# Seven query blocks of 476 instead of six of 496 and one of 351, with the block end and the projections moved to other steps

## Chip, cores, metric

One core of one Trainium2 chip. The time is device time in microseconds of one launch, the median of three runs: 10464.55 (10460.74 to 10472.15). Five engines work beside each other, each with its own queue in program order: TensorE (PE in the profile, PEld for its weight loads), VectorE (DVE), ScalarE (ACT), GpSimd (POOL) and SyncE (SP), which here only issues transfers. They meet at semaphores.

## What is computed

Two layers of a graph network on 3327 nodes with 128 features; `adj` is a dense 3327 x 3327 matrix of zeros and ones. Layer 0 (normalise, aggregate over `adj`, two linear maps, batch norm) takes the first 260 us. Layer 1 takes all the rest:

```
h = relu(layernorm(x))
q, k, v = (h @ Wq.T), (h @ Wk.T), (h @ Wv.T)       each reshaped to (128, 3327, 8)
a = einsum('dnh,dmh->dnm', q, k) * scale + adj + adj
out = softmax(a, axis=2) @ v                        for each of the 128 d
x = x + out.reshape(3327, 1024) @ Wo.T
```

So there are 128 batches (d) of an attention with 3327 queries n, 3327 keys m and a head width of only 8. The exponentials, 128 x 3327 x 3327 of them, are the bulk of the work.

## The kernel before

**Tiles.** Keys lie on the 128 partitions in 26 chunks (`NC`), queries along the free axis. Four batches (`G`) make a group, 32 groups in all. A group goes through seven query blocks (`qblocks`): six of `QB` = 496 queries and one of 351. A block goes through 13 steps (`SU`), numbered 0 to 12. A step handles four pairs; a pair is one key chunk for two of the four batches. Over a block that is 52 pairs.

**A pair** starts with a product on TensorE (`product`, L727): two matmuls of 32 contracted rows, written to one PSUM tile `s` of two banks. There are three such tiles in rotation. Then it goes one of two ways:

- *plain* (36 of 52): VectorE adds the adjacency tile `at` (L837, `d<-at,s`), and ScalarE takes the exponential of all plain pairs of a step in one instruction (`late`, L879, `d<-d`), issued in the next step behind that step's first exponential;
- *weighted* (16 of 52): ScalarE takes the exponential straight from PSUM (L846, `f<-s`), and GpSimd multiplies it by a tile `wt` of exponentials of the adjacency (L849), which were made once and lie in the DRAM tensor `wd`. The tiles `f` rotate over five buffers (pool `exf`).

A step has three plain pairs and one weighted; in the three steps of `DOUBLE` = (1, 6, 10) it has two of each. In the step after such a step the first product of the following step is issued early (`coming`).

**Weighing.** Three steps later (`LAG`) the four results of a step are multiplied with v on TensorE (L610, `av<-d,v` and `av<-f,v`, 16 matmuls, half of them in `second(0)`, half in `second(1)`) and summed into one of two accumulator banks `av`, used by the blocks in turn.

**The order inside a step** is written out by hand in the loop: first weighted exponential, `late()` of the step before, first add, `second(0)`, `step()`, second add, third add or second weighted pair (there also `begin`), `second(1)`, `go_on`.

**Block end.** The last weighing of a block is issued in step 2 of the next one. From there `step()` drives the generator `finish` by one piece a step: in step 3 VectorE copies the bank to `avs` (L618); in step 4 TensorE transposes it in four matmuls (L625), back into the same bank; in step 5 VectorE forms the reciprocal of the sums and multiplies (L632, L633, L635); in step 6 SP stores the result to `att`.

**Projections and outputs.** While group i runs, the q, k and v of group i + 2 are made in six parts and the output rows of group i - 1 in three. `begin` issues the matmul (L207) or the transposes (L268) or the last matmuls (L276) of one part in each double step, into the bank that is free; `go_on` issues VectorE's copy of it (L213, L233, L235, L270, L281) at the end of the same step, and the store a step later. GpSimd splits q and k in two (L236, L237). Groups 30 and 31 have no projections, group 0 has two sets of them and no output.

**Transfers.** All loads of `at` and `wt` are issued on SP two steps ahead (`fetch`), together with q, k, v of the next group and, in group 0, with the loads and stores that make `wd` for the next block (`more_weights`). Before the first block SP stores x to `xd` (L597) and h to `hd` (L549).

Of the kernel before, what the change touches and what calls it, by code (L numbers as in the profile page):

```python
# [9 lines left out]
F32 = mybir.dt.float32  # L10
# [3 lines left out]
ALU = mybir.AluOpType  # L14
# [4 lines left out]
N = 3327  # L19
D = 128  # L20
H = 8
P = 128
NC = 26
T = N * D
NP = NC * P
NB = 512
QB = 496
G = 4
EPS = 1e-5
HALF = 0.5 / math.sqrt(D)  # L30
# [2 lines left out]
WC = 18  # L33
CH = 4 * NP // D
NG = D // G
DOUBLE = (1, 6, 10)

# [8 lines left out]
def tile_two_layer_gnn(  # L46
# [17 lines left out]
    nc = tc.nc  # L64
# [3 lines left out]
    }))  # L68
    blocks = [(n0, min(NB, N - n0)) for n0 in range(0, N, NB)]

    qblocks = [(n0, min(QB, N - n0)) for n0 in range(0, N, QB)]

    const = ctx.enter_context(tc.tile_pool(name="const", bufs=1))
    dram = ctx.enter_context(tc.tile_pool(name="dram", bufs=1, space=DRAM))
# [10 lines left out]
    v1 = dram.tile([TP, H + 1], F32, name="v1")  # L85
    att = dram.tile([TP, H], F32, name="att")

    wd = dram.tile([NC - WC, P, N], F32, name="wd")
    xd = dram.tile([NP, D], F32, name="xd")
    hd = dram.tile([P, NP], F32, name="hd")  # L90

# [3 lines left out]
    attb = att[:T].rearrange("(d n) h -> d n h", n=N)  # L95
# [23 lines left out]
    LAG = 3  # L119
# [168 lines left out]
    def drive(part, bank=None):  # L288

        if bank is not None:  # L290
            next(part)
            part.send(bank)
        else:
            next(part, None)


    with tc.tile_pool(name="l0", bufs=1) as l0, tc.tile_pool(
        name="l0adj", bufs=3
    ) as ap, tc.tile_pool(name="l0s", bufs=2) as sp, tc.tile_pool(
        name="l0last", bufs=1  # L300
# [124 lines left out]
        for c in range(NC):  # L425
# [16 lines left out]
            i = c - 2 * NQ - 5  # L442
# [80 lines left out]
        def relu(i):  # L523
            n0, w = blocks[i]
            s = slice(n0, n0 + w)
            nc.scalar.activation(A2[:, s], A2[:, s], AF.Relu, bias=shift, scale=scale)

        def residual(i):
            pt, cs = turned(i, A, acc[i])
            nc.vector.tensor_add(xs[:, cs, :], xs[:, cs, :], pt)  # L530

        def second_norm(i, engine):

# [80 lines left out]

    def finish(rp, av, d0, n0, w):

        avs = rp.tile([P, NB], F32, name="avs")
        nc.vector.tensor_copy(avs[:, :w], av[:, :w])  # L618
        yield

        J = 4 if w == QB else 3
        R = w // J
        pt = av.rearrange("p (j q) -> p j q", j=4)
        for j in range(J):
            nc.tensor.transpose(  # L625
                pt[:R, j, :], avs[:, j : j + (R - 1) * J + 1 : J], ident
            )
        yield
        pv = pt.rearrange("p j (b h) -> p b j h", h=32)
        ri = rp.tile([P, G, 4], F32, name="ri")  # L630

        nc.vector.tensor_scalar(ri[:R, :, :J], pv[:R, :, :J, H], 1e-30, None, ALU.max)  # L632
        nc.vector.reciprocal(ri[:R, :, :J], ri[:R, :, :J])  # L633
        o = rp.tile([P, G, 4, H], F32, name="oq")
        nc.vector.tensor_tensor(  # L635
            o[:R, :, :J, :],
            pv[:R, :, :J, :H],
            ri[:R, :, :J].unsqueeze(3).to_broadcast([R, G, J, H]),
            ALU.mult,
        )  # L640
        yield
        nc.sync.dma_start(
            attb[bass.ds(d0, G), n0 : n0 + w, :].rearrange(
                "b (p j) h -> p b (j h)", j=J
            ),
            o[:R, :, :J, :].rearrange("p b j h -> p b (j h)"),
        )

    def rows_of(c):
        return min(P, N - c * P)  # L650

    def attention():


        with tc.tile_pool(name="adj", bufs=4) as ap, tc.tile_pool(
            name="adw", bufs=3
        ) as wp, tc.tile_pool(name="wk", bufs=2) as wk, tc.tile_pool(
            name="exf", bufs=5
        ) as fp, tc.tile_pool(name="exd", bufs=4) as ep, tc.tile_pool(
            name="res", bufs=2  # L660
        ) as rp, tc.tile_pool(name="psc", bufs=3, space=PSUM) as psc, tc.tile_pool(
# [7 lines left out]
            if True:  # L669
# [35 lines left out]
                def fetch(x):  # L705
                    while wanted and wanted[0][0] <= x:
                        _, kind, i, y, c = wanted.pop(0)
                        n0, w = qblocks[y]
                        if kind:
                            a = wp.tile([P, NB], F32, name="wt")  # L710
                            nc.sync.dma_start(a[:, :w], wd[c - WC, :, n0 : n0 + w])
                        else:
                            a = ap.tile([P, 2, NB], F32, name="at")
                            n = min(2, WC - 2 * c)
                            nc.sync.dma_start(
                                a[:, :n, :w], adjr[:, 2 * c : 2 * c + n, n0 : n0 + w]
                            )
                        have[kind, i, y, c] = a

                def product(i, y, c, half):  # L720
                    q, k, _ = sets[i % 2]
                    n0, w = qblocks[y]
                    we = w + w % 2
                    p = psc.tile([P, 2, NB], F32, name="s")
                    for x in range(2):
                        rs = slice(64 * half + 32 * x, 64 * half + 32 * x + 32)
                        nc.tensor.matmul(  # L727
                            p[:, x, :we], k[rs, c, :], q[rs, n0 : n0 + we],
                            start=True, stop=True,
                        )  # L730
                    return p
# [8 lines left out]
                def more_weights(i, y, s):  # L740

                    k, phase = s // 3, s % 3
                    if i or y + 1 >= len(qblocks) or k > 3:
                        return
                    n0, w = qblocks[y + 1]
                    c = WC + 2 * k
                    n = min(2, NC - c)
                    if phase == 0:
                        have["w"] = wk.tile([P, 2, NB], F32, name="t4")
# [65 lines left out]
                for x, (i, y, s) in enumerate(steps):  # L815
# [15 lines left out]
                    d = ep.tile([P, 3, 2, NB], F32, name="d")  # L831
                    es = [d[:, j] for j in range(len(plain))]

                    def add(j, p):
                        c = plain[j][0]

                        nc.vector.scalar_tensor_tensor(  # L837
                            d[:, j, :, :w],
                            have[0, i, y, c // 2][:, c % 2, :w]
                            .unsqueeze(1).to_broadcast([P, 2, w]),  # L840
                            SAFE / 2, p[:, :, :w], ALU.min, ALU.add,
                        )

                    def weighted(c, p):
                        f = fp.tile([P, 2, NB], F32, name="f")
                        nc.scalar.activation(  # L846
                            f[:, :, :w], p[:, :, :w], AF.Exp, scale=2.0
                        )
                        nc.gpsimd.tensor_tensor(  # L849
                            f[:, :, :w], f[:, :, :w],  # L850
                            have[1, i, y, c][:, :w].unsqueeze(1).to_broadcast([P, 2, w]),
                            ALU.mult,
                        )
                        es.append(f)
# [40 lines left out]
    def attention_shifted():  # L895

        with tc.tile_pool(name="shq", bufs=1) as shp, tc.tile_pool(
# [11 lines left out]
            with tc.For_i(0, D, G) as d0:  # L909
# [3 lines left out]
                for b in range(G):  # L913
# [2 lines left out]
                        sT[:, bass.ds((d0 + b if b else d0) * N, N)],  # L916
                    )
                for y, (n0, w) in enumerate(qblocks):
                    we = w + w % 2
                    av = avs2[y % 2]  # L920
                    waiting = []
# [166 lines left out]
```

## Time and profile before

| | |
|---|---|
| median of three runs | 10464.55 us |
| the profiled execution, its own time | 10472.29 us |
| its span, first to last instruction | 10470.4 us |
| granted TensorE clock, mean | 0.988 |
| first weighted exponential | 259.9 us |
| group 0, from there | 415.5 us |
| groups 1 to 31 | 311 to 317 us each |
| from the last step's first exponential to the end | 26.8 us |

Busy records of TensorE are modelled and those of ScalarE and VectorE overlap a little, so lengths are best read from start to start. In a timeline row, the first number is the start, the second the time from the first start to the last end of the merged instructions, `xN` their count, and the bracket says how long the engine had idled before it and who ended that. A group's row has busy time, mean ns of one, then the idle time in front.

### The profile page before, as it was taken

Reading aid. Unit: us, or ns where it says so; the run is one execution under the profiler, and the core shown is the slowest. Engines: PE = TensorE matmul, PEld = TensorE weight load, DVE = VectorE, ACT = ScalarE, POOL = GpSimd, SP = SyncE. Lnnn points to the kernel's source line nnn. Section 1 sums busy time; section 2 is a strip of 40 time slices with the busy share of each in tenths; the row PEclk is TensorE's granted clock in tenths of the full one; section 3 lists DMA queues with packets and bytes.
Section 4 is the critical chain, followed back from the end, with each engine's and each line's share of the span. In section 5 each row is a group of like instructions: output and inputs, shape, how many; then the busy total and the mean of one; then the engine's idle time right before and its main releaser. Section 6 shows DMA issues by size and latency. Waiting matters only on the chain.

```text
span 10470.4 us, 188308 instructions
## 1 busy us (share of the span) xinstructions
PE 9899.3 (95%) x72399; PEld 2827.8 (27%) x72399; DVE 9326.7 (89%) x9501; ACT 10000.4 (96%) x6655; POOL 8421.2 (80%) x4315
## 2 busy tenths in 40 slices
PE   7899999999999999999999999999999999999998
PEld 3222222222222222222222222222222222222222
DVE  5689999999999999999989999999999999999988
ACT  4799999999999999999999999999999999999998
POOL 1678888888888888888888888888888888888887
PEclk9899999999999999999999999999999999999999
DMA  6665666665666665666655666665666656666554
GB/s 229 207 176 157 166 168 165 164 164 159 163 168 164 167 163 156 165 170 166 166 160 156 167 170 166 163 163 156 169 169 165 165 158 161 168 168 165 158 154 127
DMA packets 1118973, 1735.29 MB, mean 166 GB/s; under 512 B 197582, under 2 KB 1094732, under 8 KB 1110380
## 3 DMA queue, kind: packets, MB, share of 16 engines
q1 hardware_dynamic: 1113678, 1718.96, 60.3%
q8 instruction: 568, 9.31, 0.4%
q10 hardware_dynamic: 4350, 4.20, 0.1%
q14 instruction: 345, 2.83, 0.1%
q0 software_dynamic: 32, 0.00, 0.0%
HBM read 1620.53 MB, written 102.30 MB: 165 GB/s over the span
## 4 chain that ended last, share of the span: by engine, by line
PE 36%; POOL 19%; DVE 18%; ACT 13%; issue 10%; DMA 1%; SPq 0%; ACTq 0%; DVEq 0%; POOLq 0%
PE av L610 18%; POOL f L849 18%; DVE d L837 16%; PE s L727 15%; ACT f L846 9%; ACT d L879 4%; PE av L625 1%; DVE avs L618 1%; POOL o L237 1%; PE av L276 1%; DMA wt<-wd 1%; DVE ri L633 0%; DMA t<-in_adjT 0%; PE av L207 0%; POOL o L236 0%
## 5 line engine op out<-in xcount | busy, mean ns | idle before, releaser
L837 DVE SCALAR_TENSOR_TENSOR d<-at,s 128x992 f32<-128x992 f32 x8064 | 8781.5, 1140 | 963.8 <-PE s L727 686.5
L849 POOL TENSOR_TENSOR f<-f,wt 128x992 f32<-128x992 f32 (+1 forms) x3584 | 7926.0, 2229 | 1786.2 <-ACT f L846 1749.5
L879 ACT ACTIVATE d<-d 128x2976 f32<-128x2976 f32 (+1 forms) x2912 | 7010.3, 2407 | 101.5 <-DVE d L837 97.0
L610 PE MATMUL av<-d,v 128*9 128x496 f32 x32256 | 5094.2, 569 | 0.8 <-ACT d L879 0.8
L727 PE MATMUL s<-q,k 32*128 32x496 f32 x23296 | 4260.4, 477 | 505.0 <-DVE d L837 259.2
L846 ACT ACTIVATE f<-s 128x992 f32<-128x992 f32 (+1 forms) x3584 | 3382.9, 966 | 166.8 <-PE s L727 85.4
L727 PEld LDWEIGHTS s<-q,k 32*128 32x128 f32 x23296 | 1786.6, 182 | 5767.2 <-DVE d L837 3267.4
L610 PE MATMUL av<-f,v 128*9 128x496 f32 x14336 | 2862.6, 568 | 0.0
L610 PEld LDWEIGHTS av<-d,v 128*9 128x9 f32 x32256 | 583.9, 88 | 1306.7 <-issue 1291.6
L610 PEld LDWEIGHTS av<-f,v 128*9 128x9 f32 x14336 | 316.8, 88 | 153.9 <-issue 148.0
L191 POOL CAST k<-ks 128x256 fp32r<-128x256 f32 x434 | 283.5, 653 | 0.0
L429 PE MATMUL acc<-a,A 128*128 128x512 f32 (+1 forms) x364 | 151.5, 569 | 23.3 <-ACT A L363 23.0
L625 PEld LDWEIGHTS av<-ident,avs 128*124 128x124 f32 (+1 forms) x864 | 122.4, 208 | 178.8 <-issue 177.5
L237 POOL TENSOR_TENSOR o<-pf,o 104x512 fp32r<-104x512 f32 x124 | 159.9, 1289 | 9.9
L625 PE MATMUL av<-ident,avs 128*124 128x128 f32 (+1 forms) x864 | 165.0, 312 | 0.6 <-DVE avs L618 0.6
L618 DVE COPY avs<-av 128x496 f32<-128x496 f32 (+1 forms) x224 | 144.8, 646 | 3.5 <-PE av L610 3.5
L436 DVE TENSOR_REDUCE amax<-a 128x1 f32<-128x3327 f32 x26 | 93.7, 3612 | 35.4 <-DMA a<-in_adj 35.2
L429 PEld LDWEIGHTS acc<-a,A 128*128 128x128 f32 x364 | 69.0, 192 | 108.2 <-issue 84.4
L402 POOL TENSOR_TENSOR sq<-wk 128x512 f32<-128x512 f32 x2 | 2.1, 1040 | 102.2 <-PE aside L403 102.2
L433 ACT ACTIVATE junk<-a 128x3327 bf16<-128x3327 f32 x26 | 77.4, 2977 | 6.6 <-DMA a<-in_adj 6.5
L236 POOL CAST o<-pf 104x512 fp32r<-104x512 f32 x124 | 76.3, 615 | 0.0
L635 DVE TENSOR_TENSOR oq<-av,ri 124x128 f32<-124x128 f32 (+1 forms) x224 | 64.2, 287 | 7.7
(120 smaller groups left out, 958.8 us busy)
## 6 DMA issues: line engine op xcount, KB each, us to landing
at<-in_adjT SPq DMA_DIRECT2D x1728, 496.0 KB
wt<-wd SPq DMA_DIRECT2D x1536, 248.0 KB
at<-in_adjT SPq DMA_DIRECT2D x288, 351.0 KB
ks<-kT SPq DMA_DIRECT2D x496, 104.0 KB
q<-qT SPq DMA_DIRECT2D x496, 104.0 KB
wt<-wd SPq DMA_DIRECT2D x256, 175.5 KB
a<-in_adj SPq DMA_DIRECT2D x26, 1663.5 KB
kT<-o SPq DMA_DIRECT2D x128, 208.0 KB
```

The source lines that it names most:

```text
L191: nc.gpsimd.tensor_copy(k[:, c : c + n, half * 64 : half * 64 + 64], ks.bitcast(F32).rearrange("g (p c) -> g c p", c=NC)[:, c : c + n, :],)
L237: nc.gpsimd.tensor_tensor(o[:CH, 1], f[:CH], o[:CH, 0].bitcast(F32), ALU.subtract)
L276: nc.tensor.matmul(bank[:CH, :D], tT[:, e, :CH], wo[:, e, :], start=(e == 0), stop=(e == H - 1))
L429: nc.tensor.matmul(acc[i][:, :w], A[:, c, :], a[:, n0 : n0 + w], start=(c == 0), stop=(c == NC - 1),)
L610: nc.tensor.matmul(av[32 * b : 32 * b + H + 1, :w], tiles[2][:, b, c, :], e, start=first, stop=last,)
L618: nc.vector.tensor_copy(avs[:, :w], av[:, :w])
L625: nc.tensor.transpose(pt[:R, j, :], avs[:, j : j + (R - 1) * J + 1 : J], ident)
L727: nc.tensor.matmul(p[:, x, :we], k[rs, c, :], q[rs, n0 : n0 + we], start=True, stop=True,)
L837: nc.vector.scalar_tensor_tensor(d[:, j, :, :w], have[0, i, y, c // 2][:, c % 2, :w] .unsqueeze(1).to_broadcast([P, 2, w]), SAFE / 2, p[:, ...
L846: nc.scalar.activation(f[:, :, :w], p[:, :, :w], AF.Exp, scale=2.0)
L849: nc.gpsimd.tensor_tensor(f[:, :, :w], f[:, :, :w], have[1, i, y, c][:, :w].unsqueeze(1).to_broadcast([P, 2, w]), ALU.mult,)
L879: nc.scalar.activation(flat, flat, AF.Exp, scale=2.0)
```

## The change

`QB` becomes 476, so that all blocks have it but the last, which is 472 wide and reaches over the 3327 queries to the padded 3328; the tiles of the attention shrink from 512 to 476 columns. `exf` has six buffers. `DOUBLE` is (3, 7, 11). `step()` is called in the steps of `PARTS` = (3, 5, 7, 8) only, after all products of the step: copy in step 3, transposes in step 5, reciprocal in step 7, store in step 8. `begin` is called in steps 7 and 11 alone, behind `second(1)`, and its bank is that of the other block. `finish` always works with four interleaved columns; the last block stores its last three rows on their own. In layer 0 x is stored to `xd` in three pieces, two of them earlier, and h to `hd` from GpSimd's queue. The adjacency's transpose is padded in both directions.

```diff
-QB = 496
+QB = 476
...
-DOUBLE = (1, 6, 10)
+DOUBLE = (3, 7, 11)
+PARTS = (3, 5, 7, 8)
...
-    qblocks = [(n0, min(QB, N - n0)) for n0 in range(0, N, QB)]
+    qblocks = [(n0, min(QB, NP - n0)) for n0 in range(0, NP, QB)]
...
-    wd = dram.tile([NC - WC, P, N], F32, name="wd")
+    wd = dram.tile([NC - WC, P, NP], F32, name="wd")
...
+        def keep_nodes(cs):
+            nc.sync.dma_start(
+                xd.rearrange("(c p) d -> p c d", p=P)[:, cs, :], xs[:, cs, :]
+            )
+
         def residual(i):
             pt, cs = turned(i, A, acc[i])
             nc.vector.tensor_add(xs[:, cs, :], xs[:, cs, :], pt)
+            if i < 2:
+                keep_nodes(cs)
...
             s = slice(4 * i0 * P, min(NC, 4 * i1) * P)
-            nc.sync.dma_start(hd[:, s], B2[:, s])
+            nc.gpsimd.dma_start(hd[:, s], B2[:, s])
...
-        nc.sync.dma_start(xd.rearrange("(c p) d -> p c d", p=P), xs)
+        keep_nodes(slice(8, NC))
         keep_columns(0, NQ)
...
     def finish(rp, av, d0, n0, w):
 
-        avs = rp.tile([P, NB], F32, name="avs")
-        nc.vector.tensor_copy(avs[:, :w], av[:, :w])
+        J = 4
+        R = -(-w // J)
+        avs = rp.tile([P, QB], F32, name="avs")
+        nc.vector.tensor_copy(avs[:, : R * J], av[:, : R * J])
         yield
 
-        J = 4 if w == QB else 3
-        R = w // J
...
+        r, j = divmod(min(w, N - n0), J)
         nc.sync.dma_start(
-            attb[bass.ds(d0, G), n0 : n0 + w, :].rearrange(
+            attb[bass.ds(d0, G), n0 : n0 + r * J, :].rearrange(
                 "b (p j) h -> p b (j h)", j=J
             ),
-            o[:R, :, :J, :].rearrange("p b j h -> p b (j h)"),
+            o[:r].rearrange("p b j h -> p b (j h)"),
         )
+        if j:
+            nc.sync.dma_start(
...
-            name="exf", bufs=5
+            name="exf", bufs=6
...
                 def begin(i, y, s):
-                    if extra:
+                    if extra and s in DOUBLE[1:]:
                         begun.append(extra.pop(0))
-                        drive(begun[0], avs2[(i * len(qblocks) + y + (s > LAG)) % 2])
+                        drive(begun[0], avs2[(i * len(qblocks) + y + 1) % 2])
...
                     second(0)
-                    step()
                     add(1, product(i, y, *plain[1]))
                     if len(rest) > 1:
                         weighted(rest[1][0], product(i, y, *rest[1]))
-                        begin(i, y, s)
                     else:
                         add(2, product(i, y, *plain[2]))
-
-                    if s - 1 in DOUBLE:
+                    if s in PARTS:
+                        step()
+
+                    if s - 1 in DOUBLE and x + 1 < len(steps):
                         coming = first(x + 1)
                     second(1)
+                    begin(i, y, s)
                     go_on(i, y, s)
...
-        "adjT": padded(adj.T),
+        "adjT": np.pad(adj.T, (0, NP - N)),
```

More of the change, by code (lines that the diff above doesn't have):

```diff
@@ L615, in finish @@
     def finish(rp, av, d0, n0, w):
-        avs = rp.tile([P, NB], F32, name="avs")
-        nc.vector.tensor_copy(avs[:, :w], av[:, :w])
+        J = 4
+        R = -(-w // J)
+        avs = rp.tile([P, QB], F32, name="avs")
+        nc.vector.tensor_copy(avs[:, : R * J], av[:, : R * J])
         yield
-        J = 4 if w == QB else 3
-        R = w // J
-        pt = av.rearrange("p (j q) -> p j q", j=4)
+        pt = av.rearrange("p (j q) -> p j q", j=J)
         for j in range(J):
@@ L629, in finish @@
         pv = pt.rearrange("p j (b h) -> p b j h", h=32)
[L630 to L634, printed above, removed]
+        ri = rp.tile([P, G, J], F32, name="ri")
+        nc.vector.tensor_scalar(ri[:R], pv[:R, :, :, H], 1e-30, None, ALU.max)
+        nc.vector.reciprocal(ri[:R], ri[:R])
+        o = rp.tile([P, G, J, H], F32, name="oq")
         nc.vector.tensor_tensor(
-            o[:R, :, :J, :],
-            pv[:R, :, :J, :H],
-            ri[:R, :, :J].unsqueeze(3).to_broadcast([R, G, J, H]),
+            o[:R], pv[:R, :, :, :H], ri[:R].unsqueeze(3).to_broadcast([R, G, J, H]),
             ALU.mult,
@@ L641, in finish @@
         yield
+        r, j = divmod(min(w, N - n0), J)
         nc.sync.dma_start(
-            attb[bass.ds(d0, G), n0 : n0 + w, :].rearrange(
+            attb[bass.ds(d0, G), n0 : n0 + r * J, :].rearrange(
                 "b (p j) h -> p b (j h)", j=J
             ),
-            o[:R, :, :J, :].rearrange("p b j h -> p b (j h)"),
+            o[:r].rearrange("p b j h -> p b (j h)"),
         )
+        if j:
+            nc.sync.dma_start(
+                attb[bass.ds(d0, G), n0 + r * J : n0 + r * J + j, :].rearrange(
+                    "b (o j) h -> o b (j h)", o=1
+                ),
+                o[r : r + 1, :, :j, :].rearrange("p b j h -> p b (j h)"),
+            )
     def rows_of(c):
@@ L709, in fetch @@
                         if kind:
-                            a = wp.tile([P, NB], F32, name="wt")
+                            a = wp.tile([P, QB], F32, name="wt")
                             nc.sync.dma_start(a[:, :w], wd[c - WC, :, n0 : n0 + w])
                         else:
-                            a = ap.tile([P, 2, NB], F32, name="at")
+                            a = ap.tile([P, 2, QB], F32, name="at")
                             n = min(2, WC - 2 * c)
@@ L748, in more_weights @@
                     if phase == 0:
-                        have["w"] = wk.tile([P, 2, NB], F32, name="t4")
+                        have["w"] = wk.tile([P, 2, QB], F32, name="t4")
                         nc.sync.dma_start(
@@ L830, in attention @@
                     plain, rest = pairs(s)
-                    d = ep.tile([P, 3, 2, NB], F32, name="d")
+                    d = ep.tile([P, 3, 2, QB], F32, name="d")
                     es = [d[:, j] for j in range(len(plain))]
@@ L844, in weighted @@
                     def weighted(c, p):
-                        f = fp.tile([P, 2, NB], F32, name="f")
+                        f = fp.tile([P, 2, QB], F32, name="f")
                         nc.scalar.activation(
@@ L918, in attention_shifted @@
                 for y, (n0, w) in enumerate(qblocks):
+                    w = min(w, N - n0)
                     we = w + w % 2
```

## The prediction

> **What bounds the kernel now.** I read the engines' shares first, then the costliest groups, then the timelines of ScalarE, VectorE and TensorE through one block of 496 queries.
>
> ```profile
> PE 9899.3 (95%) x72399; PEld 2827.8 (27%) x72399; DVE 9326.7 (89%) x9501; ACT 10000.4 (96%) x6655; POOL 8421.2 (80%) x4315
> ...
> L837 DVE SCALAR_TENSOR_TENSOR d<-at,s 128x992 f32<-128x992 f32 x8064 | 8781.5, 1140 | 963.8 <-PE s L727 686.5
> L849 POOL TENSOR_TENSOR f<-f,wt 128x992 f32<-128x992 f32 (+1 forms) x3584 | 7926.0, 2229 | 1786.2 <-ACT f L846 1749.5
> L879 ACT ACTIVATE d<-d 128x2976 f32<-128x2976 f32 (+1 forms) x2912 | 7010.3, 2407 | 101.5 <-DVE d L837 97.0
> L846 ACT ACTIVATE f<-s 128x992 f32<-128x992 f32 (+1 forms) x3584 | 3382.9, 966 | 166.8 <-PE s L727 85.4
> ```
>
> Three engines stand above 89%, so shares do not decide. The busy time of ScalarE's two groups adds to 10393 us, more than its 10000: records overlap, and what counts is the distance from start to start.
>
> ```profile
> 5322.45 1.00 ACT L846 ACTIVATE f<-s 128x992 f32<-128x992 f32 x1
> 5323.32 2.70 ACT L879 ACTIVATE d<-d 128x2976 f32<-128x2976 f32 x1
> 5325.90 1.01 ACT L846 ACTIVATE f<-s 128x992 f32<-128x992 f32 x1
> 5326.77 2.71 ACT L879 ACTIVATE d<-d 128x2976 f32<-128x2976 f32 x1
> 5329.35 1.91 ACT L846 ACTIVATE f<-s 128x992 f32<-128x992 f32 x2
> 5331.10 1.90 ACT L879 ACTIVATE d<-d 128x1984 f32<-128x1984 f32 x1
> 5332.88 1.01 ACT L846 ACTIVATE f<-s 128x992 f32<-128x992 f32 x1
> ...
> 5343.74 0.98 ACT L846 ACTIVATE f<-s 128x992 f32<-128x992 f32 x1
> 5345.13 2.69 ACT L879 ACTIVATE d<-d 128x2976 f32<-128x2976 f32 x1 [0.41 <-DVE d L837]
> ```
>
> A plain step (three adds) takes 3.45 us (5322.45 to 5325.90) for two exponentials of 3968 elements; a step with two adds, which I call double, has a second exponential on GpSimd's side and takes 4.33 (5325.90 to 5330.23: the row at 5329.35 merges this second one and the first of the next step, 0.88 later); the step after it 2.65 here, 2.63 at best. Nothing idles: ScalarE is the bound. A block without loss is 7 x 3.454 + 3 x 4.33 + 3 x 2.635 = 45.1 us. The block starts in this timeline (5089.66, 5135.50, 5182.30, 5228.63, 5276.04, 5322.45, 5368.58, 5404.84) give 45.8, 46.8, 46.3, 47.4, 46.4, 46.1 and 36.3: 315.2 us a group. So some 12 us a group are lost, and the last lines show how: the exponential of step 5 waits for VectorE.
>
> ```profile
> 5321.79 6.67 DVE L837 SCALAR_TENSOR_TENSOR d<-at,s 128x992 f32<-128x992 f32 x6
> 5329.12 1.19 DVE L837 SCALAR_TENSOR_TENSOR d<-at,s 128x992 f32<-128x992 f32 x1 [0.66 <-PE s L727]
> 5330.96 3.50 DVE L837 SCALAR_TENSOR_TENSOR d<-at,s 128x992 f32<-128x992 f32 x3 [0.65 <-PE s L727]
> 5334.38 0.67 DVE L618 COPY avs<-av 128x496 f32<-128x496 f32 x1
> 5334.96 3.38 DVE L837 SCALAR_TENSOR_TENSOR d<-at,s 128x992 f32<-128x992 f32 x3
> ```
>
> Adds follow each other after 1.098 us, so a plain step takes VectorE 3.29 of ScalarE's 3.45: 0.16 to spare. The copy of the block end (0.58 start to start) stands in plain step 3, the reciprocal's three instructions (0.70: 5342.07 to 5342.77) in plain step 5. Neither fits: steps 4 and 6 of this block take 3.85 and 4.86 instead of 3.45 and 4.33, and step 5 3.53. That is 1.0 us a block. After the double step VectorE idles 0.66 and 0.65.
>
> **The change, part by part.**
>
> *Width.* Columns of a group go from 3327 to 3328, with the same number of instructions. Per plain step ScalarE saves 8 x 20 elements; the 351 block's plain step (5371.79 to 5374.28, 2.49; 2.51 in others) against 3.454 gives 145 x 8 elements in 0.95 us, so 0.82 ns an element. Plain 3.454 - 0.13 = 3.32, double 4.33 - 0.167 = 4.164, after it 2.63 - 0.10 = 2.53; a block 7 x 3.32 + 3 x 4.164 + 3 x 2.53 = 43.35, seven less 0.35 for the last (472 wide) 303.05. The old widths without loss: 6 x 45.1 + 32.7 = 303.3. So width alone gives nothing; the gain can only be the 12 us of losses.
>
> [...]
>
> *Block end.* The copy moves to step 3, the reciprocal to step 7, both double now, after two adds. At 476 VectorE ends the second add 2.40 after the step's first exponential and gets the next step's product at about 3.0 (3.22 at 496). The copy (0.57) fits; the reciprocal's 0.70 ends at 3.10, and the second idle time of 0.65 takes the 0.1. Cost 0, against 1.0 before. Without this cover it would be 0.57 + 0.70 a block.
>
> The four transposes move from step 4 to step 5, behind that step's last product.
>
> ```profile
> 5337.57 0.73 PE L625 MATMUL av<-ident,avs 128*124 128x128 f32 x4
> 5338.23 0.50 PE L727 MATMUL s<-q,k 32*128 32x496 f32 x4
> ```
>
> They hold TensorE 0.66 from start to start. The step's last product waits for the exponential of its own step and starts 1.15 after this (5351.23 to 5352.39 in step 8; 1.12 at 476), takes 0.41, then come the weighing (0.95 from 5323.93 to 5324.88; 0.91 at 476) and the product for step 6, whose reader starts 0.53 after it (5330.42 to 5330.96): 1.12 + 0.41 + 0.91 + 0.53 = 2.97 of 3.32, 0.35 free. With 0.66 more, ScalarE waits 0.31. Seven blocks: 2.2 us a group. Bounds 0 (TensorE catches up) and 0.66.
>
> *Projections and outputs* (nine parts a group) start only in steps 7 and 11, now behind the last weighing. All write the other accumulator bank. In step 7 that bank is read by the reciprocal's last instruction in the same step, so in the changed program the projection's matmul carries a wait for VectorE; in step 11 it carries none. Behind it on TensorE stand the next step's first two products, and for them wait ScalarE and VectorE. Today's rows for matmul and copy:
>
> ```profile
> 5159.07 1.10 PE L207 MATMUL av<-wq,hj 128*104 128x512 f32 x2
> 5160.11 0.59 PE L610 MATMUL av<-d,v 128*9 128x496 f32 x2
> ...
> 5160.42 0.75 DVE L235 TENSOR_SCALAR pf<-av,low_half 104x512 f32<-104x512 f32 x1
> ```
>  Step 7, from its first exponential: second add until 2.40, reciprocal's end 3.18, matmul 3.24 to 4.27 (1.04 from 5159.07 to 5160.11), product of step 8 to ScalarE at 4.83 instead of 4.17: 0.66 late. VectorE's copy starts 1.35 after the matmul at 4.59 and takes 0.67, then three adds until 8.5, and step 8's large exponential starts at 8.6 instead of 7.53: **1.05 us**. In step 11 the matmul starts at 2.35 and the copy ends at 4.4; adds end at 7.6: 0.17. Outputs by the same count: transposes in step 7 0.5, in step 11 0.1, the eight matmuls and the sum 0.87. A group: 3 x 1.05 + 3 x 0.17 + 1.47 = 5.15. Bounds: 0.8 (all but step 11 hidden) and twice this. The stores of these parts and of the block end move with them on SP, each still one step after its producer, behind loads fetched two steps ahead: nothing. A second store of the last block's three rows (once a group) is one issue on SP, about 0.4 us there, hidden.
>
> *Sixth tile.* ScalarE waits for a free f in the step after a double one wherever a projection delays weighing (0.23 in the timeline at 5164.5); this goes. It is in the 12 us.
>
> *Start.* The hd store leaves SP for GpSimd and xd is split. SP's queue shows 7.53 us at the hd store (249.60) before the first load at 257.22; the first add starts at 265.75. By the row up to 7.5 us can go. [...] Two thirds of xd still stand in front. I take 4. On GpSimd the store stands before the k copies, which wait until 254 anyway. Group 0 loses about 100 us more than others, mostly waits on transfers; that stays, and I take -2 there.
>
> **Sum** against the profiled execution (span 10470.4, time 10472.3). Groups 1 to 29: 303.05 + 2.2 + 5.15 = 310.4; groups 30 and 31, without projections, 306.75. Together 29 x 310.4 + 2 x 306.75 = 9615 against 9771 now (all 31): -156. With -2 and -4: -162. The median is 7.7 below the profiled time; the same difference from it gives 10464.5 - 162 = **10303 us**.
>
> **Rivals.** (a) *Step 7's wait is hidden*: if VectorE's second idle time takes it, 5.15 falls to 0.8: 4.35 x 31 = 135 us more, 10168; with the transposes hidden too, 10100. For it: VectorE's idle 1.3 us. Against: reciprocal, wait and copy together are 2.8 us. (b) *The cover is only half there*: half of the 1.27 us moved work plus more lag, 0.35 a block, 78 us: 10381. For it: projections in double steps show today. (c) *Slower*: the block end in the double step is not hidden at all, since the post-double step's first product comes early and each delay of an add goes to ScalarE: 1.27 x 7 = 8.9 us a group, 10303 + 285 = 10588. It decides from 5.1 a group, 0.73 a block, on. Against: the two idle times just shown. (d) *No change*: the losses move to the new places one for one, 315 a group.
>
> **How the numbers follow.** The likeliest case 0.55 at 10303 (its own range 10240 to 10360), (a) 0.25, (b) 0.12, (c) 0.05, (d) 0.03. The range from 10150 to 10400 leaves out the low third of (a), (c) and (d). About 0.2% is what a measurement here can tell from no change; faster than that 0.93, within it 0.03, slower 0.04.
>
> **What would show it.** Right: plain steps of 3.32, no wait of ScalarE for VectorE after steps 3 and 5, no wait for a free f; step 8 of the first three blocks some 1 us long, step 6 0.3 late behind the transposes; first add near 262; 310 us a group. Wrong if adds stay above 1.1 us start to start, if ScalarE waits after step 3, or if the first three blocks are as short as the last two.

## The result, and the profile after

The changed kernel takes 10385.85 us (median of four runs, 10384.17 to 10387.67) against 10465.16 for the kernel before (now also four runs, 10460.74 to 10472.15): a ratio of 0.9924 [0.9906, 0.9941], 79 us faster. The prediction was 10303, with a range of 10150 to 10400: the direction was right and the time lies in the range, but over half of the forecast gain, 162 us, is missing. The profiled execution took 10386.0 us, its span is 10384.2, its granted clock 0.991.

The shares of the engines and the costliest groups after the change:

```profile
PE 9816.7 (95%) x72431; PEld 2888.6 (28%) x72431; DVE 9331.0 (90%) x9501; ACT 9925.5 (96%) x6655; POOL 8443.5 (81%) x4316
...
L852 DVE SCALAR_TENSOR_TENSOR d<-at,s 128x952 f32<-128x952 f32 x8064 | 8754.4, 1140 | 606.2 <-PE s L742 447.7
L864 POOL TENSOR_TENSOR f<-f,wt 128x952 f32<-128x952 f32 (+1 forms) x3584 | 7944.8, 2235 | 1680.6 <-ACT f L861 1660.7
L895 ACT ACTIVATE d<-d 128x2856 f32<-128x2856 f32 (+1 forms) x2912 | 7055.5, 2423 | 12.5 <-DVE d L852 2.3
L861 ACT ACTIVATE f<-s 128x952 f32<-128x952 f32 (+1 forms) x3584 | 3436.4, 980 | 224.7 <-PE s L742 220.9
```

The last two rows tell the story. ScalarE's idle time ahead of the large exponentials, nearly all of it for VectorE's adds, fell from 101.5 us to 12.5. Its idle time ahead of the weighted exponentials, where it waits for a product of TensorE, rose from 85.4 to 220.9. (The idle time is only a part of a loss: where ScalarE runs late by less than its records overlap, 0.10 to 0.14 us in the timeline below, the row shows nothing. The sizes below are therefore taken from start to start.)

The timeline of ScalarE through the second block of the sixteenth group, from step 5 to the start of step 8:

```profile
5108.59 0.99 ACT L861 ACTIVATE f<-s 128x952 f32<-128x952 f32 x1
5109.44 2.63 ACT L895 ACTIVATE d<-d 128x2856 f32<-128x2856 f32 x1
5112.74 0.96 ACT L861 ACTIVATE f<-s 128x952 f32<-128x952 f32 x1 [0.67 <-PE s L742]
5113.60 2.58 ACT L895 ACTIVATE d<-d 128x2856 f32<-128x2856 f32 x1
5116.07 0.96 ACT L861 ACTIVATE f<-s 128x952 f32<-128x952 f32 x1
5116.92 2.58 ACT L895 ACTIVATE d<-d 128x2856 f32<-128x2856 f32 x1
5119.39 0.96 ACT L861 ACTIVATE f<-s 128x952 f32<-128x952 f32 x1
5120.70 0.96 ACT L861 ACTIVATE f<-s 128x952 f32<-128x952 f32 x1 [0.35 <-PE s L742]
5121.56 1.78 ACT L895 ACTIVATE d<-d 128x1904 f32<-128x1904 f32 x1
```

Step 5 starts at 5108.59 and step 6 at 5112.74: 4.15 us where a plain step without loss has 3.33 (5112.74 to 5116.07, step 6). Step 7 is 5116.07 to 5120.70: 4.63 instead of the 4.16 of a double step. TensorE over the same time:

```profile
5109.76 0.49 PE L742 MATMUL s<-q,k 32*128 32x476 f32 x4
5110.18 1.14 PE L633 MATMUL av<-ident,avs 128*119 128x128 f32 x4
5111.24 0.57 PE L618 MATMUL av<-d,v 128*9 128x476 f32 x2
...
5112.16 0.48 PE L742 MATMUL s<-q,k 32*128 32x476 f32 x4
...
5119.09 1.10 PE L208 MATMUL av<-wq,hj 128*104 128x512 f32 x2 [0.61 <-DVE oq L643]
5120.12 0.49 PE L742 MATMUL s<-q,k 32*128 32x476 f32 x4
```

The four transposes (L633) hold TensorE from 5110.18 to 5111.24, 1.06 us, where before they held it 0.66; the product of step 6 (5112.16) comes 0.40 later for it. The projection (L208) stands 0.61 idle for VectorE's last instruction of the reciprocal (L643), and the next product stands behind it.

By place, averaged over groups 1 to 29, the losses against steps without loss are:

| place | us a group, predicted | measured |
|---|---|---|
| step 5 of seven blocks, transposes | 2.2 | 5.6 |
| steps 7 and 9 of blocks 0 to 2, projections | 3.15 | 2.07 |
| step 11 of blocks 0 to 2, projections | 0.51 | 0 |
| blocks 3 and 4, outputs | 1.47 | 1.7 |
| elsewhere | 0 | 0.2 |
| a group: 303.05 and these | 310.4 | 312.6 |

(The blocks are numbered from 0. Block 4's part is the last output; it alone costs 1.55.) The first weighted exponential starts at 258.2 instead of 259.9, group 0 takes 412.6 instead of 415.5; but in the executions of the kernels below group 0 takes 405 to 420 us, so this last difference says nothing.

### The profile page after: what moved, and what is told of

It reads as the page before. It is cut to its first block, busy times and chain, and to the rows that moved or that the text cites. A ratio compares the mean times of both kernels' runs of the same rounds, so it can differ in the third digit from the quotient of the medians.

```text
span 10384.2 us, 188013 instructions
## 1 busy us (share of the span) xinstructions
PE 9816.7 (95%) x72431; PEld 2888.6 (28%) x72431; DVE 9331.0 (90%) x9501; ACT 9925.5 (96%) x6655; POOL 8443.5 (81%) x4316
## 4 chain that ended last, share of the span: by engine, by line
POOL 21%; PE 16%; ACT 8%; issue 5%; DVE 3%; DMA 0%; POOLq 0%; ACTq 0%; SPq 0%; DVEq 0%
POOL f L864 20%; PE av L618 8%; PE s L742 6%; ACT f L861 5%; ACT d L895 3%; DVE d L852 2%; PE av L633 1%; POOL k L192 1%; PE av L208 1%; PE av L277 0%; POOL o L238 0%; POOL o L237 0%; DVE oq L643 0%; DVE ri L641 0%; DVE avs L628 0%
## 5 line engine op out<-in xcount | busy, mean ns | idle before, releaser
L864 POOL TENSOR_TENSOR f<-f,wt 128x952 f32<-128x952 f32 (+1 forms) x3584 | 7944.8, 2235 | 1680.6 <-ACT f L861 1660.7
L852 DVE SCALAR_TENSOR_TENSOR d<-at,s 128x952 f32<-128x952 f32 x8064 | 8754.4, 1140 | 606.2 <-PE s L742 447.7
L895 ACT ACTIVATE d<-d 128x2856 f32<-128x2856 f32 (+1 forms) x2912 | 7055.5, 2423 | 12.5 <-DVE d L852 2.3
L618 PE MATMUL av<-d,v 128*9 128x476 f32 x32256 | 5072.3, 567 | 1.9 <-ACT d L895 1.9
L742 PE MATMUL s<-q,k 32*128 32x476 f32 x23296 | 4108.3, 476 | 407.9 <-ACT f L861 334.1
L861 ACT ACTIVATE f<-s 128x952 f32<-128x952 f32 (+1 forms) x3584 | 3436.4, 980 | 224.7 <-PE s L742 220.9
L618 PE MATMUL av<-f,v 128*9 128x476 f32 x14336 | 2853.4, 566 | 0.0
L633 PE MATMUL av<-ident,avs 128*119 128x128 f32 (+1 forms) x896 | 241.3, 392 | 0.8 <-DVE avs L628 0.8
L633 PEld LDWEIGHTS av<-ident,avs 128*119 128x119 f32 (+1 forms) x896 | 198.2, 292 | 52.7 <-issue 51.1
L628 DVE COPY avs<-av 128x476 f32<-128x476 f32 (+1 forms) x224 | 144.6, 645 | 4.5 <-PE av L618 4.5
```

Of the source, the lines that this page charges most:

```text
L618: nc.tensor.matmul(av[32 * b : 32 * b + H + 1, :w], tiles[2][:, b, c, :], e, start=first, stop=last,)
L628: nc.vector.tensor_copy(avs[:, : R * J], av[:, : R * J])
L633: nc.tensor.transpose(pt[:R, j, :], avs[:, j : j + (R - 1) * J + 1 : J], ident)
L742: nc.tensor.matmul(p[:, x, :we], k[rs, c, :], q[rs, n0 : n0 + we], start=True, stop=True,)
L852: nc.vector.scalar_tensor_tensor(d[:, j, :, :w], have[0, i, y, c // 2][:, c % 2, :w] .unsqueeze(1).to_broadcast([P, 2, w]), SAFE / 2, p[:, ...
L861: nc.scalar.activation(f[:, :, :w], p[:, :, :w], AF.Exp, scale=2.0)
```

## The experiments

Two theories were set against each other for step 5, and two for step 7.

**A: the transposes are slow because they load 119 columns**, an odd count, and not because of where they stand. Rows of weight loads, groups with shapes kept apart, of before and then of after (mean ns behind the comma):

```profile
L625 PEld LDWEIGHTS av<-ident,avs 128*124 128x124 f32 x768 | 104.5, 204 | 151.7 <-issue 151.7
L625 PEld LDWEIGHTS av<-ident,avs 128*117 128x117 f32 x96 | 17.8, 244 | 27.1 <-issue 25.8 <-DVE avs L618 1.3
```

```profile
L633 PEld LDWEIGHTS av<-ident,avs 128*119 128x119 f32 x768 | 181.5, 309 | 44.0 <-issue 44.0
L633 PEld LDWEIGHTS av<-ident,avs 128*118 128x118 f32 x128 | 16.7, 195 | 8.7 <-issue 7.1 <-DVE avs L628 1.6
```

One load of 119 columns takes 309 ns, one of 118 in the same kernel 195. Block 0's step 5, in which the 472-wide block with its 118 rows is transposed, takes 3.81 us on average, that of the other blocks 4.14 to 4.22. **Its rival:** it is the place, so that the transposes should move. The first experiment pads the rows to 120, the second leaves 119 and moves the transposes to step 4, behind the first weighing. The third, for step 7, issues the reciprocal ahead of the step's first add (**C: the projection waits for the reciprocal**; the rival: the delay is the projection's own 1.04 us of TensorE). The fourth has the old steps with everything else of the change.

*Rows padded to an even number (all diffs are against the changed kernel, if nothing else is said):*

```diff
         R = -(-w // J)
-        avs = rp.tile([P, QB], F32, name="avs")
+        R += R % 2
+        avs = rp.tile([P, QB + 4], F32, name="avs")
```

> The changed kernel with the transposes of the block end on 120 rows instead of 119 (avs four columns wider, the copy 480 instead of 476). Theory A (the weight load of an odd number of columns is what costs: in the changed kernel's trace the four transposes stand 0.22 us apart on 119 rows and 0.11 on 118, and step 5 is 0.82 us too long behind 119 rows, 0.45 behind 118): transposes 0.11 to 0.12 apart, step 5 at about 3.75 us in all blocks, 0.4 us x 6 blocks x 32 groups = 77 us less than the changed kernel, about 10310. Theory B (only the place of the transposes costs, behind a product that waits for ScalarE): no difference from the changed kernel, 10386.

10315.47 us (10306.62 to 10318.72), ratio to the kernel before 0.9853 [0.9836, 0.9869]: 70 us less than the changed kernel. Step 5 falls to 3.73 to 3.80 in blocks 1 to 6, a group to 310.2: A holds for these 70 us, but a loss of 0.41 to 0.51 stays in step 5. The row of the loads falls to that of 124 columns:

```profile
L634 PEld LDWEIGHTS av<-ident,avs 128*120 128x120 f32 x768 | 102.4, 199 | 43.9 <-issue 43.9
```

*Transposes in step 4, ahead of the second and third product's adds:*

```diff
-PARTS = (3, 5, 7, 8)
+PARTS = (3, 7, 8)
...
                     second(0)
+                    if s == 4:
+                        step()
```

> The changed kernel with the transposes (still 119 rows) in step 4, between the first weighing and the second product, where the trace shows TensorE idle for 0.54 and then 0.37 us waiting for ScalarE. Theory B (the place costs): the idle 0.9 us take nearly all of the transposes' 1.06; of step 5's 0.82 some 0.15 stay: 0.67 x 7 x 32 = 150 us less than the changed kernel, about 10236. Theory A alone (the odd weight load costs wherever it stands): no more than a fifth of that, above 10350.

10296.26 us (10291.63 to 10299.42), 0.9835 [0.9819, 0.9852]: 90 us less, not the 150 of the place alone, and more than A alone would allow. Step 5 falls to 3.32 in block 0 and 3.45 to 3.62 in the others, but step 7 rises: from 4.63 to between 4.91 and 4.99 in blocks 0 to 2, and by 0.22 and 0.29 in blocks 3 and 4. VectorE's timeline, one block from step 4 on:

```profile
5069.23 10.65 DVE L852 SCALAR_TENSOR_TENSOR d<-at,s 128x952 f32<-128x952 f32 x10 [1.18 <-PE s L742]
```

It idles 1.18 us for a product that stands behind the slow transposes, and then makes ten adds without a gap. At 1.056 an add it gains 0.15 a plain step on ScalarE, so it is still late in step 7. That this lateness is the 0.2 to 0.35 added there is argued from this row; what was run is the version with both edits, below, where it is gone.

*The reciprocal ahead of the first add of step 7:*

```diff
+                    if s == 7:
+                        step()
                     add(0, product(i, y, *plain[0]))
...
-                    if s in PARTS:
+                    if s in PARTS and s != 7:
                         step()
```

> The changed kernel with VectorE's reciprocal part of step 7 ahead of the step's first add instead of behind its second, so that the bank is free before TensorE comes to the projection. Theory C (step 7's loss is the projection's matmul waiting for the reciprocal): step 7 falls from 4.62 to about 4.2 in the first three blocks, step 9 from 3.5 to 3.35, step 7 of the fifth block from 5.51 to about 4.4: 3 x 0.6 + 1.2 = 3 us a group, 95 us less than the changed kernel, about 10290. Theory D (the matmul itself, 1.04 us of TensorE in front of the next step's first product, costs that much): no gain, 10386, and since the first add is 0.7 later perhaps a loss.

10313.56 us (10304.12 to 10316.52), 0.9851 [0.9834, 0.9867]: 72 us less, of 95 expected; the miss is in the fifth block, whose step 7 falls from 5.51 to 4.84 and not to 4.4. Step 7 of blocks 0 to 2 takes 4.16, the time of a double step without loss, step 9 3.35 instead of 3.52. C holds: with nothing to wait for, the projection's own time on TensorE costs ScalarE next to nothing (0.03 in step 9). Step 5 keeps its loss; the first exponential of step 6 waits behind the transposes:

```profile
5125.44 0.97 ACT L861 ACTIVATE f<-s 128x952 f32<-128x952 f32 x1 [0.69 <-PE s L742]
```

*The old steps, with the new widths, tiles and start:*

```diff
-DOUBLE = (3, 7, 11)
+DOUBLE = (1, 6, 10)
...
-                    if extra and s in DOUBLE[1:]:
+                    if extra:
...
-                        drive(begun[0], avs2[(i * len(qblocks) + y + 1) % 2])
+                        drive(begun[0], avs2[(i * len(qblocks) + y + (s > LAG)) % 2])
...
                     second(0)
+                    step()
...
                         weighted(rest[1][0], product(i, y, *rest[1]))
+                        begin(i, y, s)
...
-                    if s in PARTS:
-                        step()
...
                     second(1)
-                    begin(i, y, s)
```

> The changed kernel's widths, six f tiles, block end code and start, with the old steps: DOUBLE (1, 6, 10), one piece of the block end in each of steps 3 to 6 behind the first weighing, projections in every step with two adds ahead of the second weighing. By the prediction's count (the loss lies in the steps, width alone brings nothing): each block keeps 1.0 us of block end, projections and outputs some 1 to 2 us a group, so 303 + 7 + 1.5 = 311.5 to 313 us a group, 10350 to 10400, no better and no worse than the changed kernel. Theory E (the sixth tile and the equal widths are the whole gain of the change, and the new steps cost): under 10350. Theory F (the new steps are the whole gain): 10440 to 10465.

10466.62 us (10460.68 to 10471.8), 0.9997 [0.9989, 1.0006]: no gain, where 10350 to 10400 was expected; it fits what that text calls theory F. By itself it says that the moved steps make the whole gain. But these transposes, too, load 119 columns, and step 4, where they stand in this order, is 4.29 us long on average. A later run undoes that (below).

*All three edits together* (rows even, transposes in step 4, reciprocal first):

> The changed kernel with all three edits: transposes on 120 rows, transposes in step 4 ahead of its second product, reciprocal ahead of step 7's adds. Alone they brought 71, 90 and 72 us. If the three losses are separate and the second run's rest (step 5 still 0.12 to 0.3 too long, step 7 0.3 longer) came from the 1.06 us that 119 rows take of TensorE: step 5 at 3.35, step 7 at 4.2, only the fifth block's step 7 longer by 0.7: 305 us a group, 240 us less than the changed kernel, 10140 to 10160. If the transposes in step 4 make VectorE late whatever they take, with the reciprocal then in front of its adds: 308 us and more a group, above 10220.

10141.25 us (10140.13 to 10142.69), 0.9689 [0.9673, 0.9705]: 245 us less than the changed kernel, while the three edits alone gave 70, 90 and 72, 232 in all. In groups 1 to 29 the gains simply add up (2.4, 2.8 and 2.6 us a group alone, 7.9 together), and most of the rest of the difference lies in group 0. Groups take 304.8 against the ideal 303.05. ScalarE's timeline, from step 3 to the start of step 6, in the second block of the sixteenth group:

```profile
4986.63 0.96 ACT L862 ACTIVATE f<-s 128x952 f32<-128x952 f32 x1
4987.47 2.59 ACT L900 ACTIVATE d<-d 128x2856 f32<-128x2856 f32 x1
4989.95 1.83 ACT L862 ACTIVATE f<-s 128x952 f32<-128x952 f32 x2
4991.64 1.82 ACT L900 ACTIVATE d<-d 128x1904 f32<-128x1904 f32 x1
4993.32 0.99 ACT L862 ACTIVATE f<-s 128x952 f32<-128x952 f32 x1
4994.16 2.62 ACT L900 ACTIVATE d<-d 128x2856 f32<-128x2856 f32 x1
4996.64 1.00 ACT L862 ACTIVATE f<-s 128x952 f32<-128x952 f32 x1
```

Step 5 (4993.32 to 4996.64) takes 3.32. On TensorE the even transposes stand ahead of step 4's second product, and not long:

```profile
4990.56 0.72 PE L634 MATMUL av<-ident,avs 128*120 128x128 f32 x4
4991.21 1.09 PE L743 MATMUL s<-q,k 32*128 32x476 f32 x6
```

They hold TensorE 0.65. None of these rows has a wait, and the total idle time of ScalarE ahead of the weighted exponentials is 28.7 us in this kernel, 224.7 in the changed one. So A and its rival both hold: of step 5's 0.82 about half is the odd count, the rest the place.

*The new steps alone, in the kernel before* (496 and 351 columns, 124 and 117 rows, five tiles, the old start):

```diff
-DOUBLE = (1, 6, 10)
+DOUBLE = (3, 7, 11)
+PARTS = (3, 5, 7, 8)
...
                     second(0)
-                    step()
...
-                        begin(i, y, s)
...
+                    if s in PARTS:
+                        step()
...
                     second(1)
+                    begin(i, y, s)
```

> The kernel before with the new steps alone: DOUBLE (3, 7, 11), block end in steps 3, 5, 7, 8 behind all products, projections in steps 7 and 11 behind the second weighing; widths 496 and 351 (transposes of 124 and 117 rows), five f tiles, old start. If the gain of the change lies in the steps and the odd row count takes half of it back: block end 0.45 in six blocks, projections and outputs 3.8 a group, the narrow block some 1.5: 303.3 + 8 = 311.5 us a group, 10340 to 10370, below the changed kernel's 10386. If equal widths and the sixth tile are what makes the steps fit: 10430 and more.

10400.33 us (10385.15 to 10404.36), 0.9931 [0.9914, 0.9948], 30 above the upper end of what was expected. Step 5 takes 3.81 to 4.03 against 3.45 without loss, although these loads have 124 columns. A second loss is in the groups' row of the weighted exponentials:

```profile
L847 ACT ACTIVATE f<-s 128x992 f32<-128x992 f32 (+1 forms) x3584 | 3398.5, 968 | 220.2 <-PE s L728 146.3 <-PE av L611 51.5 <-POOL k L192 1.5
```

51.5 us of waits for a weighing (`av`), that is for one of the five `f` to come free. The kernel before, also with five, has 40.4 us of these, the changed kernel next to none.

*Five tiles in the changed kernel:*

```diff
-            name="exf", bufs=6
+            name="exf", bufs=5
```

> The changed kernel with five f tiles instead of six. In the new order no matmul of a projection stands in front of the weighing that frees the fifth-last f, so by the order of work nothing waits: 10386, within 10 us. If the sixth tile still is worth the 0.2 us per projection seen before: 9 x 0.22 x 31 = 60 us more, 10445.

10433.99 us (10430.71 to 10445.3), 0.9971 [0.9959, 0.9982]: 48 us slower than with six. Behind a projection in step 7, ScalarE:

```profile
5144.91 0.97 ACT L861 ACTIVATE f<-s 128x952 f32<-128x952 f32 x1 [0.35 <-PE s L742]
5145.77 1.78 ACT L895 ACTIVATE d<-d 128x1904 f32<-128x1904 f32 x1
5147.89 0.96 ACT L861 ACTIVATE f<-s 128x952 f32<-128x952 f32 x1 [0.33 <-PE av L618]
```

I had expected nothing, since the projection now stands behind the last weighing of its step. Overlooked was the next one: the exponential of step 9 takes the tile that step 8's second weighing frees, and that weighing is late behind the projection. Step 8 lasts 2.8 to 3.0 in blocks 0 to 4 instead of 2.53, and step 12, behind step 11's part, 2.8 in blocks 0 to 3. What the sixth tile is worth with the old steps was not run; their timelines, in the next section, speak for no less.

*The last output part one block later* (in the version of all three edits; its large cost of 0.7 in block 4's step 7 might come from the reciprocal in the same step, so it was put into step 11):

```diff
-                    if (y, s) == (2, 12) and i:
+                    if (y, s) == (3, 8) and i:
```

> The run with all three edits, and the output rows begun one part later, so that the part with eight matmuls and VectorE's sum falls into step 11 of the fifth block and not into step 7 behind the reciprocal. If that part's loss there (0.9 us in the run with the reciprocal in front) comes from standing in the same step as the reciprocal: about 0.3 instead, 20 us less than with the three edits. If the eight matmuls themselves cost it: no difference.

10142.01 us (10137.66 to 10144.87), 0.9688 [0.9671, 0.9704]: no difference. Step 11 then takes 4.84, as step 7 did (4.89). The eight matmuls and their sum cost this in both places; the company of the reciprocal does not matter.

*121 rows, odd but more than 120, in all blocks:*

```diff
-        R = -(-w // J)
-        avs = rp.tile([P, QB], F32, name="avs")
+        R = 121
+        avs = rp.tile([P, 4 * R], F32, name="avs")
```

> The changed kernel with the transposes on 121 rows in all blocks (columns 476 to 483 of the bank are carried along and never stored). If an odd number of columns makes a weight load slow: four transposes 0.22 apart as on 119 rows, in the 472-wide block too (there 118 before), so 10386 plus 0.4 x 32 = 10 to 13 us, about 10398. If fewer than 120 columns are slow, or 119 for another reason: 0.11 to 0.12 apart and 10315 as on 120.

10408.25 us (10403.66 to 10411.69), 0.9944 [0.9928, 0.9961], 10 above the 10398 expected, with groups of 313.1 against 312.6:

```profile
L633 PEld LDWEIGHTS av<-ident,avs 128*121 128x121 f32 x896 | 215.5, 313 | 52.9 <-issue 51.2 <-DVE avs L628 1.6
```

313 ns, also in block 0, whose step 5 is now as long (4.25) as the others'. So it is not a size below some bound but, among these five, the odd count: 118, 120 and 124 columns take 195 to 204 ns, 119 and 121 take 309 and 313.

*The old steps with even rows* (the fourth experiment with the edit of the first):

> The run with the old steps (equal widths, six f tiles; it took 10466.6) with the transposes on 120 rows. If that run stood level with the kernel before only because the odd row count took back what the sixth tile and the equal widths gave: step 4 from 4.29 to about 3.85, 0.45 x 6 x 32 = 85 us less, 10380. If width and tile give nothing in the old steps: 10466.

10387.67 us (10383.61 to 10390.1), 0.9925 [0.9909, 0.9942]: 79 us below the old steps with 119 rows, and as fast as the changed kernel. Step 4 falls from 4.29 to 3.93 on average. So the "nothing" of the fourth experiment was a gain of some 79 and a loss of the same size. Set side by side:

| | 119 rows | 120 rows |
|---|---|---|
| old steps, six tiles, widths of 476 | 10466.6 | 10387.7 |
| new steps, same | 10385.9 | 10315.5 |

The steps give 81 and 72; the even rows 79 and 70.

## Why the prediction was half right

- **The steps without loss: right.** 3.32, 4.16 and 2.53 were measured where nothing disturbs them.
- **The add: 1.05 us from start to start.** The sum's chains take 3.2 us for three adds of 952 elements (4.4 to 7.6 in step 11), and no row of the kernel before shows an add of that length: its adds of 992 elements follow each other after 1.098. Three adds and a copy in VectorE's timeline:

```profile
5280.89 3.25 DVE L852 SCALAR_TENSOR_TENSOR d<-at,s 128x952 f32<-128x952 f32 x3
5284.05 0.65 DVE L628 COPY avs<-av 128x476 f32<-128x476 f32 x1
5284.78 1.15 DVE L852 SCALAR_TENSOR_TENSOR d<-at,s 128x952 f32<-128x952 f32 x1
```

 Less the last add's 1.15, two distances make 2.10: 1.05 an add, so three take 3.15 of a plain step's 3.32. The length of one record (1.15) is more than this distance.
- **The block end in double steps costs nothing: right.** In blocks without a projection ScalarE waits neither after step 3 nor after step 7; its idle time for VectorE's adds fell from 97.0 to 2.3 us.
- **The transposes in step 5: this is the step that failed.** "They hold TensorE 0.66 from start to start" was read from a row with 124 columns and carried over to 119; the term "ScalarE waits 0.31" was 0.82 to 0.93 in the six blocks with 119 columns and 0.49 in the one with 118, 5.6 us a group instead of 2.2. They hold TensorE 1.06, since a load of 119 columns takes 309 ns instead of 204; with 120 columns 70 us come back. The stated bounds of 0 to 0.66 a block did not hold it. The chain itself is the one foretold: in the rows of the changed kernel above, the last product starts 1.17 after the step does (5108.59 to 5109.76), then 0.42 to the transposes, 1.06 for them, 0.92 for the weighing and 0.58 to the exponential of step 6, together 4.15 where the prediction has 1.12 + 0.41 + 0.66 + 0.91 + 0.53 = 3.63. Of the 0.52 too little 0.40 are the transposes and 0.12 the other terms; so the slack of 0.35 was too large as well, and even with 120 columns step 5 loses 0.41 to 0.51.
- **Projections: the mechanism right, the size too large.** The wait for the reciprocal is there and 72 us hang on it. It cost 0.69 a block (0.47 in step 7, 0.2 in step 9), not 1.05; step 8 did not become 1 us longer. VectorE in step 7 of the block shown above:

```profile
5118.25 0.17 DVE L640 TENSOR_SCALAR ri<-av 119x16 f32<-119x16 f32 x1
5118.45 0.25 DVE L641 RECIPROCAL ri<-ri 119x16 f32<-119x16 f32 x1
5118.74 0.29 DVE L643 TENSOR_TENSOR oq<-av,ri 119x128 f32<-119x128 f32 x1
5120.30 0.75 DVE L236 TENSOR_SCALAR pf<-av,low_half 104x512 f32<-104x512 f32 x1 [1.27 <-PE av L208]
5120.97 1.14 DVE L852 SCALAR_TENSOR_TENSOR d<-at,s 128x952 f32<-128x952 f32 x1
```

 The reciprocal begins 2.18 after the step's start (5116.07), not 2.40, and ends 2.96 after it, not 3.18; the copy starts 1.21 after the matmul, not 1.35, and the next add 4.90 after the step's start, not 5.26. The chain is the one foretold, 0.2 to 0.4 us earlier. The outputs cost 1.7 a group instead of 1.47.
- **"Width alone gives nothing" and the sixth tile: the tile right, the width not shown alone.** Without loss the widths differ by nothing (303.05 against 303.3). Old steps with 476 columns, six tiles and even rows gain 79 us; width and tile were not run apart there. But the steps behind a double one tell where the gain sits. Step 7 of the second block of the sixteenth group, in the kernel before and then with the old steps and even rows (the first row merges step 6's second exponential and step 7's first, which starts 0.88 and 0.85 after it):

```profile
5161.00 1.87 ACT L846 ACTIVATE f<-s 128x992 f32<-128x992 f32 x2
5164.72 1.00 ACT L846 ACTIVATE f<-s 128x992 f32<-128x992 f32 x1
```

```profile
5114.27 1.80 ACT L862 ACTIVATE f<-s 128x952 f32<-128x952 f32 x2
5117.64 0.97 ACT L862 ACTIVATE f<-s 128x952 f32<-128x952 f32 x1
```

 Step 7 takes 2.84 against 2.63 without loss, and 2.52, which is without loss. Over a group such steps lose some 2.9 us in the kernel before and next to nothing with six tiles, in 31 groups some 90 us (from start to start); the exponentials that come late there start 0.08 after the weighing that frees their `f`. The width does not do this: with 476 columns and five tiles (the run above, with the new steps) such steps lose 3.3 us a group. The block end costs some 0.7 a group more than before, which the 79 us are net of. So the gain is the tile's as far as the timelines tell, and the prediction had this loss among its 12 us.
- **The start: right direction.** The queue of SP in the changed kernel:

```profile
246.63 0.42 SPq L530 DMA_DIRECT2D xd<-xs  x1
248.23 8.36 SPq L730 DMA_DIRECT2D at<-in_adjT  x1
256.64 0.48 SPq L726 DMA_DIRECT2D wt<-wd  x1
```

 The stall of 7.53 us at the `hd` store did not go with that store: the first load has one of 8.36 in its place. The first add starts at 262.79 instead of 265.75, 3.0 us earlier. But that is the best of ten: in the profiled executions with this start the first add comes between 262.8 and 265.7, in the middle at 263.7 (265.2 in the other kernel with the old start), and SP's stall at the first load is 8.2 to 9.1 us in all ten. So the start gives some 1.7 us; no run shows the 4 that the sum takes, a choice below the 7.53 of the stall.

The sum, on the profiled executions: 10472.3 to 10386.0 is 86, not 162. Of the 76 missing, groups 1 to 29 make 29 x (312.6 - 310.4) = 64 and the last two about 2 x 4 = 8: 310.7 in group 30 against 306.75; the other 4 lie at the start, in group 0 and at the end. What the groups miss is the transposes, 3.4 x 31 = 105, reduced by the smaller cost of the projections and outputs (5.15 - 3.77) x 29 = 40, with 0.2 a group on top. Rival (b), 10381, comes nearest by its number, but that is luck: its mechanism did not happen, the cover of the block end holds, and its 0.35 a block is not half of 1.27, which is 0.64. Two more sums are a little off: a block without loss is 43.32 by its own terms, not 43.35, and the gain of rival (a) cannot hold in full for the two groups without projections.

## What to carry to other kernels

A row gives the price of its own shape; when a change alters the shape of an operation, even by five columns out of 124, the row is a guess until another shape bounds it; the 117-column row, 244 ns against 204, stood in the same trace as a warning. When a part is moved next to others, list what each of its instructions must wait for and put the one that others wait for first: issuing three small VectorE instructions ahead of a step's adds instead of behind them was worth 72 us. And when an ablation shows no difference, look whether two effects cancel in it before concluding that its parts do nothing.

## What the runs showed of the hardware

- Weight loads of the transposes (fp32, every fourth column) take 195 to 204 ns for 118, 120 and 124 columns, 309 and 313 ns for 119 and 121; from one load to the next the trace has 0.111, 0.115 and 0.118 us against 0.217 and 0.222. The 117 columns of the kernel before, which lie three apart, take 244 ns, with 0.155 between them. What in the loads makes the difference, and whether it holds for columns that lie side by side, was not run.
- An add of 952 elements takes 1.05 to 1.056 us from start to start, one of 992 1.098, though a record of each lasts some 1.14 to 1.19: these records are 0.08 to 0.1 longer than the distance to the next.
- With the `hd` store moved to another queue, SP's stall did not go: 7.4 and 7.5 us at that store in the two kernels with the old start, 8.2 to 9.1 at the next load in the ten with the new one. The first add came some 1.7 us earlier in the middle, with 2.9 us between the earliest and the latest. What SP waits for there was not tried.
